# Layer 0 of a four-layer network: another order of loads, the router's sums inside a shared block, three scatters per step, fewer rows cleared, masks compared by words

## The chip, the cores and the metric

The kernel runs on one core of a Trainium2 chip. The metric is device time in microseconds (us), from launch to end, as the median of several runs. The core has five engines that work side by side: TensorE (PE, with PEld for its weight loads), VectorE (DVE), ScalarE (ACT), GpSimd (POOL) and SyncE (SP). SP issues most of the DMAs; each engine does its own instructions in order and waits on semaphores for the others.

## The reference, cut to what matters

The network takes x (2 x 1024 tokens of 256 channels), a condition vector per batch and a mask. It has four layers, each a conditional part and a feed-forward part. All the matmuls around the change are float32. Layer 0 is:

```
ys  = cond / 16
d   = rsqrt((ys*ys) @ (W*W) + 1e-8)
h   = ((x * ys) @ W) * d                      # conditional part
shared = (silu(h @ S1) * (h @ S3)) @ S2        # 512 wide, every token
logits = h @ gate_w                            # 32 experts
e      = argmax(logits); score = sigmoid(max(logits))
routed = FFN_e(h * score)                      # expert e's own three matrices, silu as above
x      = x + shared + routed
```

Layer 1 begins with an attention whose mask is a 1024 x 1024 array of bytes. If all rows of the mask are equal, the attention gives one row per batch, and the kernel has a short path for that; so it must find out, before layer 1, whether any row differs from the first.

## The kernel before, in words

Tokens stand in 16 tiles of 128 (NT = 16) or four blocks of 512 (tb = 0 to 3). XT and HT hold x and h with channels on the partitions, Xt and Ht hold them with tokens on the partitions. The weights of layer 0's experts stream through a ring of 20 pieces of 512 KB; an expert takes three pieces.

`_layer0` (from L384) does, in the order of the program:

- The loads on SP: the condition, half of xT, the conditional weight W, the router's weight, the other half of xT, the three shared matrices. Then two DMAs of `_zero_rows` (L340) clear the DRAM buffer xbuf (47 x 128 rows of 258 floats) and a part of ybuf (21 x 128 rows of 256).
- The conditional part: DVE squares W (L425), PE makes the denominators (pd, L429), then h in eight groups (ph, L441), which ACT evicts into HT with the scale (L443). ACT takes the square root (L158), and four evictions can be outstanding, since the PSUM pool has four buffers.
- The router: logits (ps_lt, L1315, then four transposes l_pl, L1325), the greatest of each row and its index (L173, L175), and `_route_static` (L550 and on): a one-hot array, running sums over the tiles (L560), two matmuls into l_R (L562, L564), a count (L567), and a chain of some twenty DVE operations that ends in the row numbers (L599). Each expert has 96 fixed rows in xbuf; tokens beyond them go to 21 spare slots.
- For each of the 16 tiles: a transpose of HT (ps_tm, L350), an eviction with the score (L455), a scatter by POOL of 128 rows to xbuf (L281). A row carries two floats more than the 256, which are set to NONE by a memset on DVE (L419). That memset covers the columns of all 16 tiles, the last of which is also the source of `_zero_rows` (`k.zero`).
- The transposes of XT into Xt (L461), and the shared feed-forward for the first two blocks: `_shared` (L1347) takes four steps per block; a step has two matmuls spg and two spu (L1374), a Silu on ACT (L1379), a product on DVE (L1383), and four matmuls spo (L1360), which are put after the next step's spg and spu. A hook may be called after each step's spo with the product `mul` and the last matmul `mm`.
- `_layer1_pre` (L645): weights of layer 1, the mask's first row in all partitions (m0), four copies on POOL that spread it (L661), four compares by bytes with the other rows (L667), four reductions (L668), a sum over partitions (l_pd, L672), and small products for layer 1.
- 24 slots of 128 rows (`Slots`, `Split`, from L1514): load the rows (xs, L297, after all scatters have landed), transpose them (ps_cm, L359), run them against the matrices of one or two experts (fpg, fpu L1670, fpt L1678, fpo L1688), write to ybuf.

Then the program reads from DVE's memory whether anything is rare (mask rows differ, or some expert overflows). On this input nothing is, and the last branch is taken: `rest` does the shared blocks 2 and 3 with gathers from ybuf (L336) in the hooks, loads of layer 1's expert matrices (L637, L641), and then the short form of layer 1.

A tile scheduler orders the instructions of each engine from the program's order, priorities and dependences; `_behind` (L1329) gives it an order without a semaphore, `_after` gives a real dependence. So small groups may stand elsewhere than in the source: the transposes of HT, for example, stand among the steps of the shared block.

Of the kernel before, what the change touches and what calls it, by code (L numbers as in the profile page):

```python
# [8 lines left out]
F32 = mybir.dt.float32  # L9
# [69 lines left out]
def _bc(ap, axis, shape):  # L79
    return ap.unsqueeze(axis).to_broadcast(shape)  # L80
# [6 lines left out]
def _consts(k):  # L87
# [23 lines left out]
    nc.vector.tensor_copy(k.iota, ii)  # L111
    nc.vector.memset(k.zero[:, 0:D], 0.0)
    nc.vector.memset(k.zero[:, D:], NONE)
    it = cp.tile([P, NT], I32, name="it")
# [150 lines left out]
class Rows:  # L265
# [30 lines left out]
    def load(self, dst, src):  # L296
        i = self.k.nc.sync.dma_start(dst, src)  # L297
        _after(self.k, i, self.new)
        self.read.append(i.ins.name)


# [37 lines left out]

def _zero_rows(k, dst):  # L340

    n, d = dst.shape[0] // P, dst.shape[1]
    return k.nc.sync.dma_start(dst.rearrange("(p r) d -> p r d", p=P), _bc(k.zero[:, 0:d], 1, [P, n, d]))


def _token_major(k, psum, src, t):

    ps = psum.tile([P, 2, P], F32, name="ps_tm", tag="t", bufs=2)
    for c in range(2):
        k.nc.tensor.transpose(ps[:, c, :], src[:, c, t * P:(t + 1) * P], k.ident)  # L350
    return ps.rearrange("p c d -> p (c d)")
# [32 lines left out]
def _layer0(k):  # L384
# [6 lines left out]
    def shared(tb, hook=None):  # L391
        po = _shared(k, pool, psum, HT, tb, *shw, hook)
        for i in range(2):
            t = tb * 4 + i * 2
            nc.vector.tensor_tensor(Xt[:, t:t + 2, :], po[i], Xt[:, t:t + 2, :], ALU.add)

    def weights(src):
        ws = [k.ring.take().rearrange("p (c f) -> p c f", f=f) for f in (F, F, D)]
        for w, n in zip(ws, ("L0_r1", "L0_r3", "L0_r2")):
            nc.sync.dma_start(w, A[n][src].rearrange("o (c p) f -> p (o c) f", p=P))  # L400
        return ws

    with ExitStack() as ctx:
# [3 lines left out]


        W, Wb0 = k.ring.take().rearrange("p (n c f) -> n p c f", n=2, c=2)
        W2, Wb1 = k.ring.take().rearrange("p (n c f) -> n p c f", n=2, c=2)  # L410
        _wload(nc, W, A["L0_cond_weight"])
        gw = rp.tile([P, 2, E], F32, name="l0_gw")
        _wload(nc, gw, A["L0_gate_w"])
        _wload(nc, XT[:, :, S:N], A["xT"][:, S:N])
        hold = []
        shw = _shared_weights(k, "L0_s1", "L0_s3", "L0_s2", F, hold)
        k.x = Rows(k, xbuf, [_zero_rows(k, xbuf)])
        k.t = Rows(k, k.tbuf, [])
        nc.vector.memset(k.Hr[:, :, D:], NONE)  # L419
        _zero_rows(k, ybuf[NS * T:(NS + NOV) * T, :])  # L420
        ys = rp.tile([P, 2, 2], F32, name="l0_ys")
# [26 lines left out]
        _logits(k, psum, rp, HT, gw, E, "l0", lg)  # L448
        m8, ixf = _top(nc, rp, lg, E, "l0")
        score = rp.tile([P, NT], F32, name="l0_score")  # L450
        nc.scalar.activation(score, m8[:, :, 0], AF.Sigmoid)
        k.x.begin()
        rows, eid, nov, end = _route_static(k, rp, k.pre, psum, ixf, E, C, NOV, "l0")
        for t in range(NT):
            nc.scalar.activation(Ht[:, t, :], _token_major(k, psum, HT, t), AF.Copy,  # L455
                                 scale=score[:, t:t + 1])
            k.x.scatter(k.Hr[:, t, :], rows[:, t:t + 1])


        for t in range(NT):  # L460
            nc.vector.tensor_copy(Xt[:, t, :], _token_major(k, psum, XT, t))  # L461

        for tb in range(2):
            shared(tb)
        _layer1_pre(k, k.pre, psum)

        rare = k.pre.tile([1, 1], F32, name="l0_raref")
        nc.vector.tensor_tensor(rare, k.differf[0:1, :], end[0:1, E - 1:E], ALU.add)
        any_ = k.pre.tile([1, 1], I32, name="l0_rare")
        nc.vector.tensor_copy(any_, rare)  # L470
        _router_biases(k, psum)

        ws = {}
        slots = Slots(k, pool, psum)
        split = Split(k, pool, psum, slots, F)
        for i in range(NS):
            lo, cols = i * T, []
            while lo < (i + 1) * T:

                e = lo // C  # L480
                if e not in ws:
                    ws[e] = weights(slice(e, e + 1))
                n = 64 if i % 3 == 1 else 32
                cols.append((slice(lo - i * T, lo - i * T + n), ws[e]))
                lo += n
            split.slot(i, cols)
        split.finish()
# [3 lines left out]
    k.l2 = _shared_pieces(k, 1024, k.l2hold)  # L491
    k.yrows = (NS + NOV) * T
    free = k.ring.i, set(k.ring.held)

    def slots_over():
        k.ring.held = set(held)
        slots = Slots(k, pool, psum)
# [11 lines left out]

        more(0)  # L510
        k.ring.i, k.ring.held = free[0], set(free[1])

    def rest():

        c = Combine(k, pool, psum, rows, Xt, XT, [0, 0] + [4] * 8, 2, 4)
        for tb in range(2, NB):
            step = c.hook(tb)

            def hook(f, mul, mm):
                if tb == 2 and f == 0:  # L520
                    _layer1_loads(k, mul)
                step(f, mul, mm)

            shared(tb, hook)
        return c.finish()
# [7 lines left out]
    with k.tc.If(rare > 0) as cmp:  # L533
# [7 lines left out]
        with cmp1.Else():  # L541
            with tc_pool(k, "l1sps", 4, PSUM) as psum:
                one(None)
    with cmp.Else():
        with tc_pool(k, "l0p", 2) as pool, tc_pool(k, "l0ps", 4, PSUM) as psum:
            one(rest())
    _layer1_add(k)


def _route_static(k, pool, keep, psum, ixf, E, C, nov, name):  # L550

# [7 lines left out]
    for t in range(NT):  # L559
        nc.vector.tensor_add(cum[:, t + 1, :], cum[:, t, :], oh[:, t, :])  # L560
    R = psum.tile([P, NT, E], F32, name=name + "_R", tag="mm")
    nc.tensor.matmul(R.rearrange("p t e -> p (t e)"), k.before,  # L562
                     oh.rearrange("p t e -> p (t e)"), start=True, stop=False)
    nc.tensor.matmul(R.rearrange("p t e -> p (t e)"), k.ones,  # L564
# [78 lines left out]


def _layer1_pre(k, pp, psum):  # L645

# [5 lines left out]
    with ExitStack() as ctx:  # L652
        pool = ctx.enter_context(tc_pool(k, "l1pr", 1))

        m0 = pool.tile([P, S], U8, name="l1_m0")
        nc.sync.dma_start(m0, A["mask"][0:1, :].to_broadcast([P, S]))

        k.mh = pp.tile([P, TB], U8, name="l1_mh")
        for g in range(4):
            q = slice(32 * g, 32 * g + 32)  # L660
            nc.gpsimd.tensor_copy(k.mh[q, :], m0[q, (g % 2) * TB:(g % 2 + 1) * TB])  # L661
        dif = pool.tile([P, 8], F32, name="l1_dif")
        for i in range(4):
            mm = pool.tile([P, 2, S], U8, name="l1_mm", bufs=2)
            nc.sync.dma_start(mm, A["mask"][i * 256:(i + 1) * 256].rearrange("(t p) s -> p t s", p=P))
            ne = pool.tile([P, 2, S], U8, name="l1_ne", tag="l1_big")
            nc.vector.tensor_tensor(ne, mm, _bc(m0, 1, [P, 2, S]), ALU.not_equal)  # L667
            nc.vector.tensor_reduce(dif[:, 2 * i:2 * i + 2], ne, AX.X, ALU.add)  # L668
        d1 = pool.tile([P, 1], F32, name="l1_d1")
        nc.vector.tensor_reduce(d1, dif, AX.X, ALU.add)  # L670
        pd = psum.tile([P, 1], F32, name="l1_pd", tag="t", bufs=2)
        nc.tensor.matmul(pd, k.ones, d1, start=True, stop=True)  # L672
        k.differf = pp.tile([P, 1], F32, name="l1_differf")
        nc.vector.tensor_copy(k.differf, pd)
        k.differ = pp.tile([P, 1], I32, name="l1_differ")
        nc.vector.tensor_copy(k.differ, k.differf)

# [33 lines left out]
        E = 16  # L711
        sim = k.sim = pp.tile([P, 2, E], F32, name="l1_sim")
        _wload(nc, sim, A["L1_sim"])
        k.gts = pp.tile([P, E], F32, name="l1_gts")
        nc.sync.dma_start(k.gts, A["L1_gates"].to_broadcast([P, E]))
        nc.scalar.activation(k.gts, k.gts, AF.Sigmoid)
        sq = pool.tile([P, 2, E], F32, name="l1_sq")
# [796 lines left out]
class Slots:  # L1514

    def __init__(self, k, pool, psum, of=None, base=0):
        self.k, self.pool, self.psum, self.of, self.base = k, pool, psum, of, base
        self.xs, self.dst = {}, {}  # L1520

    def fetch(self, i):

        if i not in self.xs:
            self.xs[i] = self.pool.tile([P, DR], F32, name="xs", bufs=4)
            self.k.x.load(self.xs[i], self.k.xbuf[i * P:(i + 1) * P, :])

# [124 lines left out]
class Split:  # L1652
# [42 lines left out]
    def slot(self, i, cols):  # L1695
# [8 lines left out]
        a = pool.tile([P, self.F], F32, name="fa", tag="sa")  # L1704
        nc.vector.tensor_mul(a, sg, pu)
        if self.old:
            self.end(self.old[0], aT, self.old[2])
        self.old = i, a, cols

    def finish(self):  # L1710
# [556 lines left out]
def kernel(ctx: ExitStack, tc: tile.TileContext, A, out):  # L2267
# [17 lines left out]
    k.Ht = k.Hr[:, :, 0:D]  # L2285
    k.zero = k.Hr[:, NT - 1, :]
    _consts(k)
    _wload(nc, k.XT[:, :, 0:S], A["xT"][:, 0:S])
    dp = ctx.enter_context(tc.tile_pool(name="rows", bufs=1, space=DRAM))
# [92 lines left out]
```

## Time and profile before

| | |
|---|---|
| runs | 1526.17, 1527.22 and 1530.15 us; median 1527.22 |
| profiled execution | 1529.61 us, span 1527.9 us |
| mean granted TensorE clock | 0.972 |
| PE idle until | 10.40 us |
| end of the shared blocks 0 and 1 | 95.5 us |
| first transposes of the slots | 101.55 us |
| slots' last matmuls (fpo) | 260.56 us |
| first scatter, last scatter | 55.91 us, 80.00 us |
| rows' first load (xs) | 84.20 us |

A line of the timeline has the start and the duration in us, the engine, the line of the kernel, the operation, output and inputs with their shapes, the number of instructions, and in brackets the idle time of the engine before them and what ended it. A window's row has the busy time of PE, PEld, DVE, ACT and POOL with the number of instructions, then the granted clock of TensorE (1.00 is full), the busy share of the DMA engines and GB/s. Each float32 matmul goes through the array in two passes, and the timeline counts passes.

### The profile page before, as it was taken

To read this page: it belongs to the slowest core of one execution; us is meant where nothing else is said; L and a number is where in the kernel's file an instruction comes from. 1 tells how busy PE (TensorE), PEld (TensorE's weight loads), DVE (VectorE), ACT (ScalarE), POOL (GpSimd) and SP (SyncE) were. 2 spreads that over 40 slices of the span, in tenths; PEclk is the share of its full clock that TensorE was granted. 3 is DMA by queue.
4 is the path that set the end of the run, shared out by engine and by line. 5 is a ranking of instruction groups with operands and counts; after the bars stand their busy time and mean duration, and the time that the engine had idled before them with its cause. 6 is when DMAs were issued, how large, how long until landed. Compare 5 with 4: busy or idle time off the path is not lost. (4 is left out here: it accounts for less than half of the span.)

```text
span 1527.9 us, 23703 instructions
## 1 busy us (share of the span) xinstructions
PE 1448.0 (95%) x8648; PEld 1025.1 (67%) x8652; DVE 479.2 (31%) x1596; ACT 304.8 (20%) x642; POOL 287.4 (19%) x317
## 2 busy tenths in 40 slices
PE   5999998999999999999999999999999969998897
PEld 2553333544556886565899999999976548864675
DVE  2742222234312444411211121211114404456432
ACT  2322221223111122211111111111112212135122
POOL 0410000300431440042010101010100253410442
PEclk9899999989999999999999999999999989998899
DMA  9879994913311763051145055246327428771470
GB/s 250 281 237 347 347 346 147 274 57 125 111 49 48 241 214 111 22 213 56 47 156 190 25 190 188 76 143 232 127 95 243 140 86 263 218 238 53 155 252 16
DMA packets 184240, 252.43 MB, mean 165 GB/s; under 512 B 17112, under 2 KB 137824, under 8 KB 184113
## 3 DMA queue, kind: packets, MB, share of 16 engines
q1 hardware_dynamic: 164448, 210.92, 42.9%
q0 software_dynamic: 14176, 36.63, 6.7%
q10 hardware_dynamic: 5488, 3.25, 0.7%
q8 instruction: 72, 1.18, 0.3%
q14 instruction: 56, 0.45, 0.1%
HBM read 284.86 MB, written 50.76 MB: 220 GB/s over the span
## 5 line engine op out<-in xcount | busy, mean ns | idle before, releaser
L281 POOL DMA_INDIRECT tbuf<-ys,sdst x114 | 112.2, 984 | 508.7 <-ACT ys L1646 382.6
L1360 PE MATMUL spo<-ring,sa 128*128 128x256 f32 x768 | 182.3, 383 | 13.8 <-DVE sa L1383 13.8
L1360 PEld LDWEIGHTS spo<-ring,sa 128*128 128x128 f32 x768 | 145.5, 191 | 63.9 <-issue 31.5
L1383 DVE TENSOR_TENSOR sa<-ssg,spu 128x512 f32<-128x512 f32 x96 | 65.8, 686 | 290.6 <-PE spu L1374 230.2
L1639 DVE TENSOR_TENSOR fa<-fsg,fpu 128x512 f32<-128x512 f32 x72 | 49.5, 688 | 316.2 <-PE fpu L1634 316.2
L1634 PE MATMUL fpg<-xsT,ring 128*128 128x128 f32 x1152 | 140.4, 275 | 0.7 <-issue 0.7
L1634 PE MATMUL fpu<-xsT,ring 128*128 128x128 f32 x1152 | 140.4, 275 | 0.0
L1634 PEld LDWEIGHTS fpg<-xsT,ring 128*128 128x128 f32 x1152 | 137.0, 192 | 2.7 <-issue 0.9
L1634 PEld LDWEIGHTS fpu<-xsT,ring 128*128 128x128 f32 x1152 | 134.4, 192 | 0.0
L1643 PE MATMUL fpo<-ring,fa 128*128 128x256 f32 x576 | 130.3, 379 | 0.0
L1379 ACT ACTIVATE ssg<-spg 128x512 f32<-128x512 f32 x96 | 57.3, 597 | 329.7 <-PE spg L1374 274.0
L1643 PEld LDWEIGHTS fpo<-ring,fa 128*128 128x128 f32 x576 | 106.7, 190 | 13.0
L1374 PE MATMUL spg<-HT,ring 128*128 128x512 f32 x192 | 95.1, 611 | 5.6 <-issue 2.9
L1374 PE MATMUL spu<-HT,ring 128*128 128x512 f32 x192 | 91.8, 599 | 0.0
L1374 PE MATMUL spg<-XT,ring 128*128 128x512 f32 x192 | 90.6, 593 | 0.1
L1374 PE MATMUL spu<-XT,ring 128*128 128x512 f32 x192 | 90.2, 592 | 0.0
L1610 PE MATMUL cph<-xsT,ring 128*128 128x128 f32 x624 | 84.2, 278 | 5.4 <-DVE sn L1538 2.3
L1610 PEld LDWEIGHTS cph<-xsT,ring 128*128 128x128 f32 x624 | 75.9, 191 | 9.7 <-issue 2.4
L1617 PE MATMUL cpo<-ring,ch 128*128 128x256 f32 x312 | 79.9, 380 | 0.0
L1638 ACT ACTIVATE fsg<-fpg 128x512 f32<-128x512 f32 x72 | 43.0, 597 | 171.7 <-PE fpg L1634 171.7
L1374 PEld LDWEIGHTS spu<-XT,ring 128*128 128x128 f32 x192 | 36.5, 190 | 45.9 <-issue 45.0
L1374 PEld LDWEIGHTS spu<-HT,ring 128*128 128x128 f32 x192 | 36.9, 194 | 44.7 <-issue 44.2
(574 smaller groups left out, 1656.3 us busy)
## 6 DMA issues: line engine op xcount, KB each, us to landing
ring<-in_L_w SPq DMA_DIRECT2D x108, 1024.0 KB
ring<-in_L_r SPq DMA_DIRECT2D x96, 512.0 KB
ring<-in_L_r SPq DMA_DIRECT2D x156, 256.0 KB
xs<-xbuf SPq DMA_DIRECT2D x138, 129.0 KB
ring<-in_L_W SPq DMA_DIRECT2D x32, 512.0 KB
yt<-tbuf SPq DMA_DIRECT2D x48, 256.0 KB
xbuf<-ACC SPq DMA_DIRECT2D x1, 6063.0 KB
ring<-in_L_s SPq DMA_DIRECT2D x6, 512.0 KB
```

Of the source, the lines that this page charges most:

```text
L281: i = k.nc.gpsimd.indirect_dma_start(out=self.ap, out_offset=bass.IndirectOffsetOnAxis(ap=idx, axis=0), in_=rows, in_offset=None, **end)
L1360: mm = nc.tensor.matmul(po[g // 2][:, g % 2, :], a[:, g * P:(g + 1) * P], W2[:, f, :], start=f == 0 and g % 2 == 0, stop=f == nf - 1, skip ...
L1374: mm = nc.tensor.matmul(ps, W[:, c, f * P:(f + 1) * P], X[:, c, cols], start=c == 0, stop=c == 1)
L1379: k.silu = nc.scalar.activation(sg, pg, AF.Silu)
L1383: mul = nc.vector.tensor_mul(a, sg, pu)
L1610: made = [nc.tensor.matmul(ph[:, f, :], R1[:, c, f * P:(f + 1) * P], xT[:, c, :], start=c == 0, stop=c == 1) for f in range(2) for c in ra ...
L1617: made = [nc.tensor.matmul(po, h[:, f, :], R2[:, f, :], start=f == 0, stop=f == 1) for f in range(2)]
L1634: made = [nc.tensor.matmul(ps[:, j, :], W[:, c, (f0 + j) * P:(f0 + j + 1) * P], xT[:, c, :], start=c == 0, stop=c == 1) for ps, W in ((pg, ...
L1638: nc.scalar.activation(sg, pg, AF.Silu)
L1639: nc.vector.tensor_mul(a[:, f0:f0 + 4, :], sg, pu)
L1643: made = [nc.tensor.matmul(po, a[:, f, :], W2[:, f, :], start=f == 0, stop=f == 4 * nh - 1) for f in range(4 * nh)]
```

## The change

- Loads: W first, then xT in four quarters, then the router's weight. Four matmuls on a tile of ones stand ahead of everything on PE. Layer 1's sim and gates are loaded here, before the clearing.
- Clearing: only the 24 x 128 rows of the fixed slots, from a source of four rows (`k.zeros`). The other 23 x 128 rows of xbuf are cleared later: in the third shared block on the usual path, or, on the rare path, ahead of the spare slots together with ybuf's, where the rows are scattered a second time.
- Router: indices and `_route_static` are called from the hook of step 0 of the first shared block; its first matmul is put behind that step's last. The transposes, evictions and scatters of three tiles follow in each hook, and two transposes of XT.
- Masks: out of `_layer1_pre` into the slots; a generator gives one 128-row block for every second slot, compared with m0 as 256 words by xor and joined by or, behind the last product of the slots.
- The first five experts' matrices are asked for before the first slot, and the first xs loads stand behind the last of them.

Its core, with the helpers:

```diff
-    _wload(nc, k.XT[:, :, 0:S], A["xT"][:, 0:S])
...
-def _zero_rows(k, dst):
-    n, d = dst.shape[0] // P, dst.shape[1]
-    return k.nc.sync.dma_start(dst.rearrange("(p r) d -> p r d", p=P), _bc(k.zero[:, 0:d], 1, [P, n, d]))
+def _zero_rows(k, dst, src):
+    n, d = src.shape[1], dst.shape[1]
+    m = dst.shape[0] // P // n
+    return k.nc.sync.dma_start(dst.rearrange("(p r) d -> p r d", p=P).rearrange("p (m r) d -> p m (r d)", r=n),
+                               _bc(src.rearrange("p r d -> p (r d)"), 1, [P, m, n * d]))
...
+        warm = psum.tile([P, 4, P], F32, name="warm0", tag="mm")
+        for _ in range(4):
+            nc.tensor.matmul(warm, k.ones, _bc(k.ones, 1, [P, 4, P]), start=True, stop=True)
...
         _wload(nc, W, A["L0_cond_weight"])
         gw = rp.tile([P, 2, E], F32, name="l0_gw")
+        for tb in range(NB):
+            _wload(nc, XT[:, :, tb * TB:(tb + 1) * TB], A["xT"][:, tb * TB:(tb + 1) * TB])
         _wload(nc, gw, A["L0_gate_w"])
-        _wload(nc, XT[:, :, S:N], A["xT"][:, S:N])
         hold = []
         shw = _shared_weights(k, "L0_s1", "L0_s3", "L0_s2", F, hold)
-        k.x = Rows(k, xbuf, [_zero_rows(k, xbuf)])
+        sim = k.sim = k.pre.tile([P, 2, 16], F32, name="l1_sim")
+        _wload(nc, sim, A["L1_sim"])
+        k.gts = k.pre.tile([P, 16], F32, name="l1_gts")
+        nc.sync.dma_start(k.gts, A["L1_gates"].to_broadcast([P, 16]))
+        k.x = Rows(k, xbuf, [_zero_rows(k, xbuf[0:NS * T, :], k.zeros)])
         k.t = Rows(k, k.tbuf, [])
-        nc.vector.memset(k.Hr[:, :, D:], NONE)
-        _zero_rows(k, ybuf[NS * T:(NS + NOV) * T, :])
+        nc.vector.memset(k.Hr[:, 0:NT - 4, D:], NONE)
...
+        def lead(f, mul, mm):
+            if f == 0:
+                ix = rp.tile([P, NT, 8], U32, name="l0_ix", tag="ix")
+                for t in range(NT):
+                    _behind(k, nc.vector.max_index(ix[:, t, :], m8[:, t, :], lg[:, t, :]), mul)
+                ixf = rp.tile([P, NT, 8], F32, name="l0_ixf", tag="ixf")
+                nc.vector.tensor_copy(ixf, ix)
+                k.x.begin()
+                got[:] = _route_static(k, rp, k.pre, psum, ixf, E, C, NOV, "l0", mm)
+            rows_of(f, mm)
+        def rows_of(n, mm):
+            for t in range(3 * n, min(3 * n + 3, NT)):
+                nc.scalar.activation(Ht[:, t, :], _token_major(k, psum, HT, t, mm), AF.Copy,
+                                     scale=score[:, t:t + 1])
+                k.x.scatter(k.Hr[:, t, :], got[0][:, t:t + 1])
+            for t in range(2 * n, 2 * n + 2):
+                stream(t, mm)
+        got = []
+        shared(0, lead)
+        rows, eid, nov, end = got
+        shared(1, lambda f, mul, mm: rows_of(4 + f, mm))
         _layer1_pre(k, k.pre, psum)
...
+        ws = {e: weights(slice(e, e + 1)) for e in range(5)}
+        slots = Slots(k, pool, psum, ref=sent[-1])
+        muls = []
+        mask = _mask_rows(k, k.pre, pool, psum, muls)
         for i in range(NS):
+            if i < 18 and i % 2 == 1:
+                next(mask)
...
+            muls.append(split.slot(i, cols))
...
+                if clear and tb == 2 and f == 1:
+                    zero = pool.tile([P, 1, DR], F32, name="l0_zero", bufs=1)
+                    _behind(k, nc.vector.memset(zero[:, :, 0:D], 0.0), mul)
+                    nc.vector.memset(zero[:, :, D:], NONE)
+                    k.x.read.append(_zero_rows(k, xbuf[NS * T:, :], zero).ins.name)
...
+def _mask_rows(k, pp, pool, psum, muls):
...
+    for i in range(8):
+        mm = pool.tile([P, S], U8, name="l1_mm", bufs=2)
+        nc.sync.dma_start(mm, A["mask"][i * P:(i + 1) * P])
+        yield
+        to = any_ if i == 0 else ne
+        _behind(k, nc.vector.tensor_tensor(to, mm.bitcast(I32), m0.bitcast(I32), ALU.bitwise_xor), muls[-1])
+        if i:
+            nc.vector.tensor_tensor(any_, any_, ne, ALU.bitwise_or)
+    d1 = pool.tile([P, 1], F32, name="l1_d1", bufs=1)
+    nc.vector.tensor_reduce(d1, any_, AX.X, ALU.max)
+    nc.vector.tensor_scalar_min(d1, d1, 1.0)
```

Here `stream(t, mm)` copies the transposed tile t of XT to Xt, `got` carries what `_route_static` returns, and `sent` lists the DMAs of the experts' matrices. In `_layer1_pre` the byte compares, and the loads of sim and gates, are gone.

## The prediction

> **What bounds the kernel now.** I read the page first: its table of engines and its row of TensorE by slices.
>
> ```profile
> PE 1448.0 (95%) x8648; PEld 1025.1 (67%) x8652; DVE 479.2 (31%) x1596; ACT 304.8 (20%) x642; POOL 287.4 (19%) x317
> ...
> PE   5999998999999999999999999999999969998897
> ```
>
> TensorE sets the time nearly everywhere. The first slice (38.2 us) is the emptiest, at 5 tenths, and the change works just there. The chain that ended last is no help: its pieces start at 1134 us. So I follow PE itself through layer 0, in the timeline (start, duration, in brackets the idle time before and what ended it):
>
> ```profile
> 10.40 1.87 PE L429 MATMUL pd<-l_ys,ring 128*128 128x2 f32 x8 [10.40 <-DVE ring L425]
> 12.12 15.82 PE L441 MATMUL ph<-XT,ring 128*128 128x512 f32 x32
> 27.88 1.92 PE L1315 MATMUL ps_lt<-HT,l_gw 128*32 128x512 f32 x16
> ...
> 30.32 0.90 PE L1325 MATMUL l_pl<-ident,l_lt 128*128 128x128 f32 x4
> 34.39 0.48 PE L350 MATMUL ps_tm<-ident,HT 128*128 128x128 f32 x1 [3.17 <-ACT ACC L455]
> 37.27 2.05 PE L562 MATMUL l_R<-l_oh,before 128*128 128x512 f32 x2 [2.41 <-DVE l_e L591]
> ...
> 43.83 2.08 PE L564 MATMUL l_R<-l_cum,ones 128*128 128x512 f32 x2 [3.04 <-DVE l_cum L560]
> ...
> 92.04 3.62 PE L1360 MATMUL spo<-ring,sa 128*128 128x256 f32 x16
> 95.49 0.28 PE L672 MATMUL l_pd<-l_d,ones 128*128 128x1 f32 x2
> ...
> 101.55 1.12 PE L359 MATMUL ps_cm<-ident,xs 128*128 128x128 f32 x4
> ```
>
> The reader sees 10.4 us with nothing, three waits for the router (8.6 us), the end of the shared blocks at 95.49, and the first slot at 101.55. The granted clock in 2 us windows (PE, PEld, DVE, ACT, POOL busy, then PEclk) tells what the waits cost beside themselves:
>
> ```profile
> 30.00:32.00 2.00, 1.20 (x8) 0.55 (x6) 1.14 (x3) 1.55 (x2) 0.00 (x0) 1.00 1.12 213
> 32.00:34.00 2.00, 0.00 (x0) 0.00 (x0) 2.00 (x23) 0.37 (x2) 0.00 (x0) 0.73 1.08 253
> ...
> 48.00:50.00 2.00, 2.00 (x6) 1.19 (x5) 1.93 (x7) 0.75 (x2) 0.00 (x0) 0.50 1.09 385
> 50.00:52.00 2.00, 2.00 (x9) 1.09 (x8) 1.70 (x5) 1.97 (x4) 0.00 (x0) 1.00 1.10 380
> ```
>
> From about 33 to 50 us PE runs at half clock, though it has been busy since 43.8. The matmuls also start slow: weight loads of ph come 0.86 us apart up to 16.2, then 0.43 (the record says 1.00 there, so I trust the spacing).
>
> **The change, part by part.** Times are those of the profiled execution: span 1527.9, time 1529.61, 2.4 above the median 1527.22 of the runs.
>
> *Order of loads.* DVE squares W at 9.65, when W has landed behind 1 MB of xT. Now W (256 KB) goes first and xT follows in four quarters. In 6 to 8 us the queue moved 406 GB/s; 1.05 MB at that rate is 2.6 us, so W is there at 7.05, and pd starts at 7.05 + 0.75 = 7.8 instead of 10.40: **2.6**. ph is not starved: a quarter takes 1.3 us to come and 3.44 (8 passes of 0.43) to use. The router's weight now lands behind xT, with some 10 us to spare. The small loads of layer 1 (sim, gates) go ahead of the clearing; gates feeds a Sigmoid on ACT between two evictions of ph, and with four PSUM buffers PE feels it only if gates lands after 22 us; behind 4 MB at 380 GB/s I expect 17. DVE's memset of four rows instead of one (0.9 for 0.27) makes the first eviction 0.6 later, under the same buffers: 0.
>
> *Warm matmuls.* Four (8 passes) need only the ones of 1.1 us. At 0.86 they last until 8.0 at most, about when W is there, so they cost nothing or 0.2. pd then takes 0.86 instead of 1.72, and ph's first 4.14 us (12.06 to 16.2, 4.8 passes) take 2.07: **2.9**. Bounds 0 (the clock falls before pd) to 2.9; I take the upper, since half clock lasted 5.8 us from 10.40 and the warm block plus pd is longer. ph then ends at 27.9 - 5.5 = 22.4.
>
> *Router inside the shared block.* The stretch 30.32 to 95.49 lasts 65.2. Its work at full clock, from rows: two shared blocks, 8 steps of 1.72 + 1.72 + 1.73 = 41.4; 64 transposes at 0.43 per four = 6.9; the router's R and count 1.8; the logits' transposes 0.45: 50.6 in all. So 14.6 us there are waits and half clock. In the built order of the changed kernel, step 0's four spg/spu matmuls and step 1's follow the logits at once; R comes after spo of step 0. What stays late next is the running sum. From spu's end at 29.0: the product 0.7, 16 max_index at 0.16 = 2.6, cast and one-hot 0.9, 2 + 14 sums at 0.22 = 3.5, with a second product between (0.7): about 37.8, while PE is ready at 35.9. ACT changes tables as often as before (four loads of 1.28); the pair around the score lies between the Silu of step 0 and that of step 1, whose input is ready at 30.7: 0. I leave a wait of 1.9 there, 1.7 for the clock (0 to 3.4, half of a stretch as long as 43.8 to 50 would cost 3), and 0.5 for transposes that wait for evictions (0.47 each on ACT, 0.42 on DVE, two buffers). The gain is 14.6 - 4.1 = **10.5**; bounds 6 to 14.6.
>
> A rule of the Trainium skill bears on this: "TensorE: Matmul & The Clock Gate", Part 1, says that the clock falls only after an idle window of about 3.4 us and rises after as long a busy one. The trace differs: 0.73 in the window 32 to 34 puts the fall near 32.9, some 1.7 us after PE went idle. By the page the wait of 1.9 costs no clock, and the forecast would be 1.7 lower.
>
> *Fewer rows cleared.* 24 x 128 rows (3.2 MB) instead of 47 x 128 plus 2.75 MB of ybuf. What it frees is seen on DVE and POOL:
>
> ```profile
> 43.62 0.09 DVE L419 MEMSET ACC<- 128x32 f32 x1 [3.33 <-DMA xbuf<-ACC]
> ...
> 60.74 2.28 DVE L667 TENSOR_TENSOR l_ne<-l_mm,l_m 128x2048 uint8<-128x2048 uint8 x1
> ...
> 61.12 2.73 POOL L281 DMA_INDIRECT xbuf<-ACC,l_rows  x1 [0.30 <-issue]
> ...
> 84.20 0.34 SPq L297 DMA_DIRECT2D xs<-xbuf  x1
> ```
>
> The memset of row names waited for the clearing and held the sums by 3.3 us; that wait is in the 14.6 already. The other 23 x 128 rows (3.0 MB) are cleared on the path actually taken in the third shared block, behind layer 1's weights on SP (landing about 304); before it, 6.2 MB took 13.2 to 43.6, so 15 us more of DMA, to 319. The next loads behind it are needed at 357 and were issued at 306 and later, so it costs 0; without that cover up to 1 (the last gather, 300.6).
>
> *Three scatters per step.* They move from one run to six groups, ahead of and around mask copies on POOL. The chain: rows are made 9.1 us after R (45.94 to 55.02), plus four evictions of xT on DVE (1.7): 39.0 + 10.8 = 49.8. Twelve scatters at 1.26 (0.96 + 0.30): 64.9. The built order has POOL's four l_mh copies here, of which the second waits for the landing (3.2, as from 80.96 to 84.19): 68.1, copies 1.9, four scatters 5.0, landing 3.2: 78.2. SP is then released for xs; 3.3 to land (as cT, 0.83 to 4.17): 81.5. Behind the waiting xs on SP stand only weights for which the ring is full (17 pieces are ahead of it). So the chain hides by 4 us under PE (85.5, below), and caps the total gain at 20.
>
> *Masks by words in the slots.* Four compares of 2.28 and four reductions of 2.27 leave DVE in 60 to 85, where PE is full: 0. Their uint8 compare also stood beside each long scatter. The 128x256 int32 xor and or are not in the trace; bounds 0.29 (eight times the elements took 2.28) to 0.69 (128x512 f32); I take 0.42, the 128x256 add of L1414. Two in every second slot, after a product that is not needed for 2.5 us, with DVE busy a quarter:
>
> ```profile
> 120.00:140.00 20.00, 19.70 (x184) 7.87 (x181) 4.09 (x8) 4.15 (x10) 0.00 (x0) 1.00 1.00 331
> ```
>
> Cost 0, up to 8 x 0.84 = 6.7 if each delayed PE in full. The masks' DMAs (1.2 MB more) meet a full queue: after 17 pieces loaded ahead, 41.4 MB of weights, 6.3 of rows in and out and 1.2 of masks remain for 161 us of slots (101.55 to 262.5), 304 GB/s, and the row above, the lowest of its stretch, moved 331 (last column). A mask load on SP waits for a xor four slots before its use. Cost 0, up to 3.
>
> **Sum.** 2.6 + 2.9 + 10.5 = 16.0: shared blocks end at 79.5, the 6.06 before the first slot stay, slots start at 85.5 instead of 101.55. All later engine orders are unchanged, so the rest shifts: 1529.6 - 16.0 = 1513.6 against the profiled execution, or **1511.2** against the median.
>
> **Rivals.**
> - *The rows come late.* The chain of scatters, not PE, opens the slots: it needs more than 85.5, that is 0.25 us more per scatter, or evictions and DVE waits hold the block by as much. For it: POOL, DVE and ACT are dense there. Against: the long scatters lose their neighbour. Gain 8 to 13: 1514 to 1519.
> - *No stall at all.* The sum is ready, the clock stays: the cap, 1505 to 1508.5.
> - *The slots stretch* by masks or DMA, by 3 to 10: 1514 to 1521.
> - *Half clock holds (the slower side).* The interleaved block is full of short waits; if these keep PE at half clock, every us of its 50.6 costs one more. 1.7 is in the sum, so from 17.7 us of work at half clock the gain is gone; held through the first block (25 us) it gives 16.0 - 23.6, or 1535. For it: 33 to 50 was at half clock. Against: 50 to 75, as interleaved with transposes, ran at 1.00.
> - *The change not doing what it says* is excluded by the built order.
>
> **Numbers.** Forecast (13 to 18.5 gained: 1508.7 to 1514.2) 0.61; rows late 0.16; no stall 0.11; slots stretched 0.04; half clock 0.08. What this measurement can tell from no change is about 0.3% (4.6 us). Faster 0.91, within 0.03 (parts of the last two), slower 0.06. The range takes the first three cases: 1504 to 1519.
>
> **What would show it.** Right: pd near 7.8 with ph 0.43 apart; R without a 3 us wait; the shared blocks ending near 79.5, the first slot at 85.5, the slots 161 long. Wrong: PEclk 0.50 for most of 35 to 60; ps_cm waiting for xs; a slot longer than 6.6.

## The result, and the profile after

The changed kernel took 1517.35 to 1522.55 us in four runs, median 1519.38; the kernel before took a median of 1528.68 in the runs beside them. The ratio is 0.9949, with a 95% interval of 0.9932 to 0.9966: 9.3 us less, where 16.0 had been forecast. The profiled execution is the slowest of the four (1522.55 us, span 1520.8); against the span of before (1527.9) it shows 7.1 us less, and that is what the lines below account for.

The page's row of engines and its row of TensorE by slices; the emptiest slice, the first, went from 5 tenths to 8:

```profile
PE 1448.3 (95%) x8660; PEld 1023.3 (67%) x8660; DVE 468.9 (31%) x1606; ACT 304.9 (20%) x642; POOL 280.9 (18%) x317
...
PE   8999998999999999999999999999999969998897
```

TensorE's timeline (columns as before: start, duration, engine, line, operation, then the wait in brackets). The front of the program did what was forecast:

```profile
7.70 1.05 PE L447 MATMUL pd<-l_ys,ring 128*128 128x2 f32 x8 [1.11 <-DVE ring L443]
8.62 13.98 PE L459 MATMUL ph<-XT,ring 128*128 128x512 f32 x32
22.53 1.92 PE L1381 MATMUL ps_lt<-HT,l_gw 128*32 128x512 f32 x16
...
34.12 1.02 PE L621 MATMUL l_R<-l_oh,before 128*128 128x512 f32 x2
...
37.42 1.12 PE L624 MATMUL l_R<-l_cum,ones 128*128 128x512 f32 x2 [1.10 <-DVE l_cum L618]
...
83.64 1.86 PE L775 MATMUL l_pu<-l_tpd,l_natq 128*128 128x16 f32 x8 [0.64 <-DVE l_tpd L767]
...
87.03 1.12 PE L364 MATMUL ps_cm<-ident,xs 128*128 128x128 f32 x4
```

pd starts at 7.70, ph ends 5.35 us earlier, and R waits 1.10 for the running sum instead of 3.04. The windows (busy time of PE, PEld, DVE, ACT, POOL, then granted clock, DMA share, GB/s) show the clock at 1.00 where before it was 0.73 and 0.50; up to the slots it now falls only in the small matmuls ahead of them (0.50 from 84 to 90 us):

```profile
32.00:34.00 2.00, 2.00 (x10) 1.58 (x9) 1.90 (x13) 0.00 (x0) 0.00 (x0) 1.00 1.09 366
...
48.00:50.00 2.00, 2.00 (x9) 1.39 (x8) 0.69 (x1) 0.00 (x0) 1.63 (x2) 1.00 1.07 361
...
84.00:86.00 2.00, 2.00 (x12) 2.00 (x11) 0.29 (x2) 0.00 (x0) 0.00 (x0) 0.50 0.00 0
...
120.00:140.00 20.00, 18.49 (x174) 7.16 (x166) 5.28 (x11) 4.03 (x9) 0.00 (x0) 1.00 0.99 336
```

The last row is one of the slots: PE is busy 18.49 of 20 us, where before it was 19.70. Here the gain was lost again. By stage:

| stage | before | after | gained |
|---|---|---|---|
| to the end of ph | 27.88 | 22.53 | 5.35 |
| to the end of the shared blocks (last spo, or the transposes behind it) | 95.66 | 79.46 | 10.85 |
| from there to the first ps_cm | 5.9 | 7.6 | -1.7 |
| slots, first ps_cm to the end of the last fpo | 160.9 | 168.0 | -7.1 |
| idle behind the slots | 2.94 | 3.47 | -0.5 |
| rest, from the third block's first spg (265.43, 258.50) | 1262.5 | 1262.3 | 0.2 |

The slot in which most was lost, in TensorE's timeline:

```profile
138.35 0.44 PE L364 MATMUL ps_cm<-ident,xs 128*128 128x128 f32 x2
140.68 0.44 PE L364 MATMUL ps_cm<-ident,xs 128*128 128x128 f32 x2 [1.90 <-DMA xs<-xbuf]
141.05 3.52 PE L1738 MATMUL fpg<-ring,xsT 128*32 128x512 f32 x16
```

The rows of the second slot of a pair are 1.90 us late, and the clock falls (0.50 in 142 to 144), so that the next 16 passes take 3.52 instead of 1.92. Before, the same pair was turned without a wait:

```profile
152.90 0.66 PE L359 MATMUL ps_cm<-ident,xs 128*128 128x128 f32 x4
```

Why the rows are late is seen by setting two engines side by side. DVE's line of the xor, then SP's queue at the same time:

```profile
131.25 0.42 DVE L723 TENSOR_TENSOR l_ne<-l_mm,l_m 128x256 int32<-128x256 int32 x1
```

```profile
131.69 0.34 SPq L720 DMA_DIRECT2D l_mm<-in_mask  x1
132.24 0.88 SPq L407 DMA_DIRECT2D ring<-in_L_r  x2
133.17 0.48 SPq L297 DMA_DIRECT2D xs<-xbuf  x1
```

The xor ends at 131.67, and SP issues the next mask load at 131.69: it stood there until the buffer was free. The row load is behind it, at 133.17, 7.5 us ahead of its use. SP's waits from 85 to 262 us (what it waited for, us in total, times, longest) have a new line, the second one below; before, no load of SP waited for DVE in the slots:

```profile
SPq L407 <- PE ps_cm L364: 32.6, 14, 4.4
...
SPq L720 <- DVE l_ne L723: 14.4, 5, 4.8
```

The same view of the kernel before has this for the first of them:

```profile
SPq L400 <- PE ps_cm L359: 31.2, 14, 5.1
```

A second new wait, of weight loads for writes to ybuf (10.2 us in five), falls behind 170 us, after both late rows, so it is not what made these late.

**Theories.** A: mask loads on SP wait for compares, and the row loads behind them come late. B: the added DVE operations delay the copies that TensorE needs. C: the other order at the start of the slots (five experts asked for ahead, row loads behind them). D: the masks' traffic fills the DMA engines. E came up later: with the masks in the slots TensorE's built order is another.

### The profile page after: what moved, and what is told of

Same layout as the page of the kernel before. It is cut to its first block, busy times and chain, and to the rows that moved or that the text cites. A ratio compares the mean times of both kernels' runs of the same rounds, so it can differ in the third digit from the quotient of the medians.

```text
span 1520.8 us, 23724 instructions
## 1 busy us (share of the span) xinstructions
PE 1448.3 (95%) x8660; PEld 1023.3 (67%) x8660; DVE 468.9 (31%) x1606; ACT 304.9 (20%) x642; POOL 280.9 (18%) x317
## 5 line engine op out<-in xcount | busy, mean ns | idle before, releaser
L1440 PEld LDWEIGHTS spu<-HT,ring 128*128 128x128 f32 x192 | 37.4, 196 | 46.7 <-issue 46.0
```

Of the source, the lines that this page charges most:

```text
L1440: mm = nc.tensor.matmul(ps, W[:, c, f * P:(f + 1) * P], X[:, c, cols], start=c == 0, stop=c == 1)
```

## The experiments

All ratios are against the kernel before on the same chip (its median was 1518 us beside e1 to e4, 1526.6 to 1528.7 beside the others). The times in the traces, in us:

| kernel | last spo of the shared blocks ends | first ps_cm | slots | third block starts | ratio (95%) |
|---|---|---|---|---|---|
| before | 95.7 | 101.6 | 160.9 | 265.4 | 1 |
| changed | 79.0 | 87.0 | 168.0 | 258.5 | 0.9949 (0.9932 to 0.9966) |
| e10 changed again | 79.2 | 87.2 | 169.3 | 260.2 | 0.9957 (0.9943 to 0.9971) |
| e1 four buffers | 77.7 | 85.7 | 163.9 | 253.2 | 0.9924 (0.9908 to 0.9941) |
| e2 no masks | 77.7 | 85.3 | 164.9 | 253.5 | 0.9906 (0.9888 to 0.9925) |
| e3 compares only | 77.7 | 84.7 | 164.4 | 252.8 | 0.9908 (0.9888 to 0.9928) |
| e4 loads only | 80.4 | 88.4 | 163.7 | 255.7 | 0.9913 (0.9892 to 0.9933) |
| e5 bytes ahead of slots | 99.7 | 107.5 | 161.7 | 272.7 | 1.0051 (1.0033 to 1.0069) |
| e6 masks alone | 103.8 | 109.2 | 164.4 | 276.6 | 1.0101 (1.0072 to 1.013) |
| e7 loads by POOL | 82.0 | 88.8 | 163.5 | 256.2 | 0.9943 (0.9922 to 0.9964) |
| e8 loads and warm alone | 91.3 | 97.3 | 162.6 | 263.8 | 0.9984 (0.9972 to 0.9997) |
| e9 masks in second block | 79.8 | 87.2 | 162.0 | 253.0 | 0.9927 (0.9908 to 0.9945) |
| e15 the same again | 77.9 | 84.9 | 161.1 | 249.5 | 0.9925 (0.991 to 0.994) |
| e12 single turns | 79.8 | 87.2 | 165.8 | 256.8 | 0.9962 (0.995 to 0.9974) |
| e13 no warm | 81.5 | 88.4 | 166.1 | 257.6 | 0.9979 (0.9964 to 0.9994) |
| e14 one buffer | 79.3 | 86.5 | 169.0 | 258.9 | 0.9959 (0.9942 to 0.9976) |

Each row of times is one execution. The rest behind the third block's start took 1259.7 to 1266.1 us in the traces of e5, e6, e8 and e9, all on one chip, so the whole times do not resolve a few us of the slots. The slots themselves contain some half clock at their start that differs by execution: the first 16 passes of fpg took 2.8 us in the kernel before and the changed one, and 3.64 in e3, e8, e9, e12, e13 and e14, where the 16 passes of fpu behind them took 0.2 to 0.7 more than 1.89 as well.

**e1: four buffers for the mask blocks.**

```diff
-    ne = pool.tile([P, S // 4], I32, name="l1_ne", bufs=1)
...
-        mm = pool.tile([P, S], U8, name="l1_mm", bufs=2)
+        mm = pool.tile([P, S], U8, name="l1_mm", bufs=4)
...
+        ne = mm.bitcast(I32)
```

> The changed kernel with four buffers for the mask blocks instead of two (the xor writes into the block itself, which frees the space). In the changed kernel the slots took 168.0 us (first ps_cm to last fpo) against 160.9 before. Theory A (a mask load on SP stands waiting for the xor two blocks earlier, and xs and weight loads stand behind it): the waits of SP for DVE (14.4 us) go, the slots take 161 to 163, the time falls by 5 to 7 to about 1513. Theory B (the added DVE operations delay the copies that TensorE needs): slots still near 168, time 1519. Theory C (the order of loads at the start of the slots: five experts ahead, xs behind them): 168, 1519. Theory D (the masks' traffic fills the DMA engines): 168, 1519.

Slots 163.9, and no mask load of SP waits for a compare there. The same row load goes out 6.0 us earlier in SP's queue (4.7, counted from the first ps_cm):

```profile
127.17 0.69 SPq L297 DMA_DIRECT2D xs<-xbuf  x1
```

TensorE turns that pair at 136.99 without a wait, 9.8 us after the issue, as in the kernel before (143.08 to 152.90). So B, C and D are not the main cause: compares, loads and the early experts are all still there, four of the eight mask loads between 120 and 165 us. But the slots stay 1 above the bound that A gave, and 3 above before; three other rows are late (0.18, 0.22 and 1.60), and the built order is another too, with ten pairs.

**e2, e3, e4: the mask's parts by themselves.** In e2 the loads and the xor of the eight blocks are deleted, in e3 the loads only (each xor takes m0), in e4 the xor and or of the blocks:

```diff
-        mm = pool.tile([P, S], U8, name="l1_mm", bufs=2)
-        nc.sync.dma_start(mm, A["mask"][i * P:(i + 1) * P])
+        mm = m0
```

> The changed kernel without the loads and compares of the mask's rows 0 to 1023 (the first row is compared with itself once; so the test for differing rows is left out). A, B and D: the slots take 161 as before, time 1512 to 1513. C: the slots keep 168 and the time 1519.

> The changed kernel with all its xor, or and reduce operations, but on the first row itself; the eight loads of mask blocks are left out, and so the test for differing rows. A and D: slots 161 to 162, time 1513. B: slots near 168, time 1519. C: 168, 1519.

> The changed kernel with the eight mask loads into two buffers, but only one xor and the reduce: the compares of the blocks are left out, so a load waits for no compare. A: slots 161 to 163, time 1513. B: slots 161. C and D: slots near 168, time 1519.

163.7 to 164.9 in all three, so the compares in the slots (e3) cost nothing beyond what the slots without masks take (e2). e4 does not test the traffic there: with nothing to wait for, the eight loads went out before the slots, the last six here:

```profile
53.73 8.87 SPq L720 DMA_DIRECT2D l_mm<-in_mask  x6
```

The traffic is tested by e7 below. But without any mask 164.9 is not 161, which A did not foretell. The built orders differ: before, eleven pairs of slots are turned together (ps_cm x4, one pair split by a wait of 0.26) and two slots singly; the changed kernel turns nine pairs and six slots singly, and l_pd, the last matmul of the masks, which e2 to e4 keep, now stands in the slots. That is theory E. Fewer pairs are not the whole of it, though: e3 has eleven pairs, in other places than before, and takes 164.4. There late rows (0.65, 0.97 and 0.34), the half clock at the start (1.4 more than before) and the wait of l_pd (0.44) make up the 3.4.

**e5: the byte compares ahead of the slots again**, with nothing else undone.

> The changed kernel with the mask part undone alone: the four compares and reductions by bytes stand ahead of the slots again. Theory A (SP's waits for the compares) and theory E (the masks in the slots change the built order of TensorE: ten slots are then turned singly instead of four, and a single turn shows up to 0.5 us of the copy to xsT twice per pair) both expect the slots at 161 as before, since here the order of the slots is that of the kernel before and no load waits for a compare; first ps_cm near 86, time about 15 below before, ratio 0.990. Theory C (five experts asked for ahead, xs behind them): slots at 164 or more, as in the kernel without masks, ratio 0.992.

The slots are at 161.7, as expected of A and E and not of C. But the kernel is slower than before. DVE's timeline:

```profile
37.56 2.28 DVE L757 TENSOR_TENSOR l_ne<-l_mm,l_m 128x2048 uint8<-128x2048 uint8 x1
39.76 0.18 DVE L615 TENSOR_TENSOR l_cum<-l_cum,l_oh 128x32 f32<-128x32 f32 x1
39.88 2.29 DVE L758 TENSOR_REDUCE l_dif<-l_ne 128x2 f32<-128x2048 uint8 x1
```

The scheduler puts the eight long operations between the running sums, each of which needs 0.18 us. On TensorE the second part of R waits for them:

```profile
57.32 2.08 PE L621 MATMUL l_R<-l_cum,ones 128*128 128x512 f32 x2 [17.12 <-DVE l_cum L615]
```

So moving the masks away from there was no separate edit of cost nothing: it is what makes room for the router's sums in the block.

**e6: the masks in the slots, on the kernel before.** The mask part of the diff alone.

> The kernel before with the mask part alone: blocks of 128 rows loaded and compared by words in every second slot. A and E: slots 167 to 168 instead of 161, first ps_cm 101 to 102, time 5 to 7 above before, ratio 1.004. If the loss needs the other parts (theory C): slots near 161 to 164, ratio 1.000 to 1.002.

Slots 164.4, that is 3.5 lost, half of what was expected, though SP's waits for l_ne are 13.3 us and nine pairs are left, as in the changed kernel. Three rows are late, by 0.99, 0.30 and 0.27, and no half clock follows. So about the same wait on SP cost far less here. The shared blocks end 8.1 later, which no theory foretold: TensorE's transposes of XT wait up to 1.7 us for nothing that the profile names ("issue") between 62 and 76 us. That cause is open.

**e8: order of loads and warm matmuls, on the kernel before.**

> The kernel before with the other order of loads and the four warm matmuls alone. From the prediction's terms: pd at 7.7, ph ends at 22.5 instead of 27.9, and everything behind it 5.4 earlier, if the clearing does not hold the router's sums longer: ratio 0.9965. If the sums wait for the clearing (which ends at 43.6 as before): only the first part of that comes through, 2 to 3, ratio 0.998 to 0.9985.

pd at 7.96, ph ends at 22.79, 5.1 earlier; the shared blocks end 4.4 earlier, the slots take 162.6, and the third block starts 1.6 earlier. The second bound came true (ratio 0.9984), but by another way: the sums did not wait longer, 4.4 of the 5.1 passed through the blocks, and 1.6 was lost in the slots and 1.0 behind them (idle 3.92 instead of 2.94).

**e9 and e15: the masks in the second shared block.**

```diff
-        shared(1, lambda f, mul, mm: rows_of(4 + f, mm))
+        muls = []
+        mask = _mask_rows(k, k.pre, pool, psum, muls)
+        next(mask)
+        def second(f, mul, mm):
+            muls.append(mul)
+            next(mask)
+            next(mask)
+            rows_of(4 + f, mm)
+        shared(1, second)
```

The five experts' loads are put ahead of the shared blocks, and the blocks have four buffers as in e1.

> The changed kernel with the xor and or of two blocks in each step of the second shared block, four buffers, xor in place; nothing of the masks is left in the slots but the row l_m. A and E: slots at 161, first ps_cm 86 to 88 (DVE has 1.7 us more per step of 5.2), ratio 0.990. C: slots 164, ratio 0.992. If DVE or the loads hold the shared block: its end moves from 79 to 81 or later.

> The masks in the second shared block again, beside the version with the loads on POOL's queue. Slots 162, ratio 0.9927 as the first time (interval 0.9908 to 0.9945); if the compares in the slots cost nothing, the other one is within 0.002 of it.

Slots 162.0 and 161.1, with the pairs of before. The block was not held (its end is 79.8 and 77.9, with 79.0 and 79.2 in the changed kernel). In e15 the slots end at 246.0, and the third block starts 16.0 earlier than before:

```profile
249.47 2.90 PE L1447 MATMUL spg<-HT,ring 128*128 128x512 f32 x3 [3.42 <-issue]
```

Both ratios, 0.9927 and 0.9925, lie below the two of the changed kernel (0.9949 and 0.9957), by about 4 us; e9 and e15 ran on other chips than the changed kernel, and the intervals overlap in part.

**e10: the changed kernel again**, on the chip of e12 to e14.

> The changed kernel itself, on the chip of the three next ones, so that they can be set beside it. Its ratio was 0.9949, interval 0.9932 to 0.9966; slots 168.0, built with twelve of 24 slots turned singly or in a broken pair. If the loss in the slots is fixed by the order of the program (theories A and E) the slots take 167 to 169 again; if it was the luck of one execution (an xs that happened to be late), 163 to 165.

Slots 169.3, late rows at the same two places (1.64 and 1.20 us) and at a third. So the loss in the slots comes again with the program; how late each row is differs (2.00 at the third place, where the changed kernel's pair took 0.98 instead of 0.66).

**e14: one buffer.** `bufs=1` for the mask blocks.

> The changed kernel with one buffer for the mask blocks instead of two: each load now waits for the xor of the block just before it, two slots later than in the changed kernel. The built order of TensorE is that of the changed kernel. Theory A: SP's waits for DVE rise from 14.4 us to some 60 (eight loads, up to 13 us each, less what SP runs ahead), xs comes later, slots at 180 or more, ratio above 1.000. Theory E alone (only the order costs): 168, ratio 0.995.

A miss for A as it was put: 169.0. SP's waits for DVE rose from 14.4 to 20.1 only, since in SP's order each load moved to the place that the next one had: up to 177 us SP's order is that of the changed kernel, and the first long wait is 3.1 in both. So the experiment did not double the wait ahead of the rows that were late. These were late at the same two places, by 1.67 and 1.65; one wait more (3.8) came behind them, at 189.42, and no row was late there. So the price doesn't go with the sum of SP's waits.

**e12: single turns.** e9 with slots 11 to 19 put behind the work of the slot before.

```diff
-        xT = self.slots.rows(i)
+        xT = self.slots.rows(i, None, self.last if 11 <= i < 20 else None)
```

> The kernel with the masks in the second shared block (slots 162.0, ratio 0.9927), with slots 11 to 19 each turned singly: their ps_cm are put behind the work of the slot before. Nothing else is changed, and SP waits for no compare. Theory E: a pair turned together takes 13.17 us, two single ones 14.1, so four and a half pairs cost 4.2: slots 166, ratio 0.9955. Theory A alone: 162 as without it.

Slots 165.8, with seven pairs instead of eleven and no late row: 3.7 more than e9 and 4.7 more than e15, for four pairs 0.9 to 1.2 each (0.9 is the better figure: e9 began its slots at half clock for as long as e12, e15 for some 0.8 less). TensorE's timeline shows where it goes:

```profile
159.79 0.44 PE L364 MATMUL ps_cm<-ident,xs 128*128 128x128 f32 x2
160.74 1.92 PE L1745 MATMUL fpg<-ring,xsT 128*32 128x512 f32 x16 [0.52 <-DVE xsT L1609]
```

A slot turned singly waits 0.52 for DVE's copy each time; a pair waits 0.30, once, and the other copy lies under the first slot's matmuls.

**e13: no warm matmuls.**

> The changed kernel without the four warm matmuls. From the prediction's terms: pd at 7.7 to 7.8 as with them, but 1.7 us long, and ph at half clock for about 4 us: ph ends 2.9 later, at 25.4 instead of 22.5; ratio 0.9949 + 0.0019 = 0.997. Rival: the clock falls between the warm matmuls and pd in any case (TensorE was idle for 1.1 us there), or rises during pd as soon: less than 1 us.

pd takes 1.87 and ph ends at 24.82 instead of 22.52 in e10: 2.3, near the first theory. The slots begin only 1.3 later than in e10, and the ratio differs by 0.0022, with intervals that overlap. The slots take 166.1, less than in e10, with the same order and SP's waits for DVE nearly as long (13.3): the same two rows are late, but by 0.99 and 0.61, and no half clock follows.

**e7: the mask loads issued by POOL.**

```diff
-        nc.sync.dma_start(mm, A["mask"][i * P:(i + 1) * P])
+        nc.gpsimd.dma_start(mm, A["mask"][i * P:(i + 1) * P])
```

> The changed kernel with the eight mask loads issued by POOL, which has nothing to do in the slots, instead of SP; the compares stay where they are. The built order has ten pairs of slots turned together and three single turns ahead of the last (changed kernel: nine pairs; before: eleven). Theory A: no row load waits behind a mask load, SP shows no wait for DVE, the slots take 162 to 164 (one pair 0.9, the waits for l_d and l_rare 1.0), ratio 0.991 to 0.993. If the compares on DVE or the masks' traffic were the cause after all: 167 or more, ratio 0.995.

Slots 163.5 with all compares in place and six of the eight loads issued between 107 and 174 us, so neither the compares nor this traffic is the main cause; the waits are now on POOL, which nobody needs:

```profile
120.59 0.57 POOL L720 DMA_DIRECT2D l_mm<-in_mask  x1 [12.57 <-DVE l_ne L723]
```

The built order has eleven pairs here, in other places than before (the expectation says ten). Two rows are still late, 1.04 and 0.86. The third block starts 2.3 earlier than in the changed kernel, though a late start cost this execution some 2.6 (last section); the ratio, 0.9943, missed the expected 0.991 to 0.993 and can't be told from the changed kernel's. So the gain of 4.5 is shown in the slots of one trace, not in the whole time.

Over all the traces: in the five kernels in which SP waits for compares in the slots (changed, e10, e14, e13, e6) the row at the fifth turn is late, by 0.99 to 1.90; in the other eleven it is not. So SP's wait makes this row late; by how much is not settled by it, since the wait of SP just ahead of it is 3.1 in all five.

## Why the prediction was wrong

- **Order of loads, 2.6, and warm matmuls, 2.9: right.** pd came at 7.70 (7.8 forecast), ph ended at 22.53 (22.4). e8 alone gives 5.1, and e13 gives 2.3 of the 2.9 to the warm matmuls.
- **Router inside the block, 10.5: right in size, 10.85.** The wait for the sum was 1.10 (1.9 forecast), and no half clock came behind it (1.7 forecast); the terms listed for the wait add up to 37.4, not 37.8, so to 1.5. Instead about a microsecond went into transposes that waited for ACT (0.94 at 65.7). It rests on the masks' move, as e5 shows, which the prediction did not see.
- **Three scatters per step, fewer rows cleared: right.** The first row load went out at 74.67, 3.5 earlier than worked out; no scatter was long. The rest of the program took 1262.3 us with the late clearing and 1262.5 before.
- **"The 6.06 before the first slot stay": too small by 1.5.** l_pu and pn ran at half clock (1.86 instead of 1.04, 1.01 instead of 0.60), since the clock now falls at about 83 us, where before it fell at the slots' start (0.80 in 100 to 102); in the first slot it is at half in both. And 0.68 went into a wait for a copy of XT.
- **"A mask load on SP waits for a xor four slots before its use. Cost 0, up to 3": the step that failed.** It asked when the mask was needed, which is never urgent, and not what stands behind the load in SP's order. Behind it stand row loads with little time in hand. The one above went out 4.7 later than in e1, counted from the first ps_cm, and came 1.90 late, so it had some 2.8 in hand (an estimate, if both take as long to land); others had none: also before, two of the pairs took 0.96 and 0.80 instead of 0.66, and one was split by a wait of 0.26. The cost was put at 0 where the late rows and the half clock behind them took 4.9. The same failure sits in "the slots 161 long", measured 168.0: "all later engine orders are unchanged" does not hold within the slots, where two pairs are gone.

How the 7.1 divides, by the trace of the changed kernel: late rows 3.3 (1.90 and 1.40); half clock behind the first, 3.52 less 1.92, 1.6; two pairs fewer at 0.94 (a pair takes 13.17, two single slots 14.1), 1.9; the wait of l_pd 0.44. That is 7.2, less the 0.26 of a late row before, 7.0. By the experiments the border is less sharp: with the pairs of before 160.9 to 162.6 (before, e5, e8, e9, e15); with another order, but no mask load that waits for a compare, 163.5 to 164.9 (e1, e2, e3, e4, e7); with both 164.4 in e6, 166.1 in e13, and 168.0 to 169.3 in the changed kernel, e10 and e14. So another order, with the late rows in it, cost 1 to 4, and SP's waits anything from nothing that shows (e6) to some 5. In e1 to e4 and e7 one row is 0.97 to 1.86 late without any such wait, each time at a later turn than the fifth; why is open, since no run changed the turns there alone.

The rival that came true, slots stretched by 3 to 10, had been given 4 in 100. Its mechanism was named, but as a matter of bandwidth, and e7 shows that traffic is not the main part. (By the prediction's own cap of 20 its case of no stall ends at 1507, not at 1505; that case did not come.)

## What to carry to other kernels

A DMA that waits in an in-order queue is paid by the loads behind it: for every load added to a queue, ask what it waits for, and how much time the next urgent load behind it has left. An edit that looks free on an engine with time to spare may be what another edit lives on, so cost edits also with the others undone. And compare the built order in the very stage that gets new instructions: here it lost two pairs at 0.94 each.

## What the runs showed of the hardware that was not expected

- The clock's fall is not a matter of the idle time alone. In e8 TensorE was idle for 1.70 us ahead of pd, and the clock stayed, as in the changed kernel (1.11); in e7 it was idle for 1.13, and the clock fell behind pd, whose matmuls are short. In the slots a wait of 1.64 (e10) or 1.65 (e14) was followed by half clock, waits of 1.67 (e14) and 2.00 (e10) were not. The windows of e7:

```profile
9.00:10.00 1.00, 1.00 (x8) 0.82 (x8) 0.91 (x6) 0.08 (x1) 0.00 (x0) 0.97 1.06 383
10.00:12.00 2.00, 2.00 (x4) 0.80 (x3) 1.80 (x12) 0.12 (x1) 0.00 (x0) 0.50 1.06 375
```

  In e4, e5 and e7, W landed about 1 us later than in the other executions with warm matmuls (pd at 8.63 to 8.78 instead of 7.67 to 8.00), and ph took 15.55 to 15.68 instead of 13.98: some 2.6 us in three of thirteen traces. The Trainium skill, "TensorE: Matmul & The Clock Gate", Part 1, calls its window free-running, so that the point of change depends on where in it the work falls; that fits two outcomes of like idle times. Its length of some 3.4 us doesn't fit as the least idle time: here 1.64 to 1.90 us without a matmul were enough in the slots, and 1.13 with the short matmuls of pd at the start.
- Behind one late row of 1.90 us, half clock cost another 1.6. So this short stall of TensorE cost almost twice its length; the one of 1.40 in the same trace cost only itself.
- The 128x256 int32 xor, or and reduce took 0.42 to 0.43 each, no more than a copy of that shape in float32 (0.42).
